# Layer 1's projections for coming units, moved to other steps of an attention unit

## The chip, the core and the metric

The kernel runs on one core of a Trainium2 chip. The core has five engines that run side by side, each with its own queue of instructions in a fixed order: TensorE (PE, matrix products, which it writes to PSUM), VectorE (DVE), ScalarE (ACT), GpSimd (POOL) and SyncE (SP, which here only issues transfers). Semaphores tie the queues together. [...] The metric is device time of one execution in microseconds.

## What is computed

Two layers act on an image of 2 x 256 x 64 x 64 in float32, that is two batches of 256 channels and 4096 places. Layer 0 is a normalised attention with four heads of 16 channels, a gate from a small convolution, and a sigmoid at its end. Layer 1, which the change touches, is

```python
qkv = jnp.einsum('oc,bchw->bohw', w_qkv, x) + b_qkv[None, :, None, None]
qkv = qkv.reshape(b, HEADS, 3 * head_dim, h * w)
q, k, v = jnp.split(qkv, 3, axis=2)
attn = jax.nn.softmax(jnp.einsum('bhdn,bhdm->bhnm', q, k) * scale, axis=-1)
out = jnp.einsum('bhnm,bhdm->bhnd', attn, v).reshape(b, c, h, w)
return jnp.einsum('oc,bchw->bohw', w_out, out) + b_out[None, :, None, None] + x
```

with four heads of 64 channels, so for each batch and head a softmax over 4096 keys for each of 4096 queries. The x here is layer 0's result.

## The kernel before

**Units.** Layer 1 works in 32 units (b, g, j): a batch b, a pair of heads g, and a block j of 512 queries. They run in that order, so unit n has n = 16 b + 8 g + j. A unit goes through the 4096 keys in 32 blocks of 128 keys, two blocks a step, thus 16 steps (`US`). Step t of the whole loop, which the code numbers on through all units, handles blocks 2t and 2t + 1; below, "step 5" is the sixth step of a unit.

**One block.** `score` (L807) makes two products, one a head, of 64 x 128 keys and 64 x 512 queries, into a pair of PSUM banks; there are two such pairs (`psp`), so the scores of a block need the pair of the block two before. `keep` takes them out: DVE folds them into a running maximum `rmax` (L824, not for the first block of a unit), and ACT copies them to SBUF as `raw` (L825). The copy stands behind the maximum. `raw` is a ring of 24 blocks.

**Groups of maxima.** The softmax uses a maximum for each query over 16 blocks (`GS`), so a unit has two groups. At a group's end, steps 8 and 16 (step 0 of the next unit), PE turns the running maximum by transposes (`turn_max`, L832), DVE reduces it (`fold`, L844), head by head through the one PSUM bank called `misc`, POOL splits the result into three bfloat16 parts (`split`, L855 to L862), PE turns those (`turn`, L871, a step later), ACT casts them (L876), and PE spreads them over the keys (`spread_shift`, L885, two steps later).

**The second half.** `LAG` is 10: ten steps after its scores, a block is shifted on DVE (L890), put through the exponential on ACT (L902), added to the row sums on POOL (`acc`, L912 for the first addition of a group, L914 after), and a step later multiplied by the values on PE (`gather`, L924). So DVE does two maxima and two shifts in a step, ACT two copies and two exps, POOL two additions, and PE four products of scores and four of values.

**The unit's end.** Steps 12 to 14 of the next unit bring the sums together on PE (`total`, L954), keep them on ACT (L962, L964), turn them and the results (`turned`, L969) and scale the results on DVE (`rows`, L995); POOL adds the halves (L1002, L1006), SP stores them (L1022).

**What comes next.** The queries of the following unit and, for the first 24 units, one block of keys and values of the next pair of heads or batch are projected in between: `next_queries` (L618, two products over the two halves of the channels, then `keep_queries` on ACT, L645), `next_keys` (L618, then `store_keys`, L760, and a store to DRAM, L763), `next_values` (L651, then `store_values`, L774, and a store, L775). Their blocks of x are fetched to one of three buffers `xb` (L614). All of them use the one `misc` bank. Units 18 to 21 carry besides, two blocks each, the output projection of the first batch: `fetch_output`, then for each half o of the output channels `project_out` (L1029, two products) and `output` (L1037 on DVE). The blocks begin at steps 0 and 8.

**The order.** It is written by hand and kept: `at(t, place, step)` hangs a piece of work on a place of a step, and the loop at the end of the kernel runs through the places. In a step PE gets the scores of both blocks, then what hangs on *early*, then the gather of two blocks, then what hangs on *late*. ACT gets the exp of the step before, the first copy, an exp, what hangs on *early end*, and the second copy. DVE gets the first maximum, a shift, *early end*, the second maximum, *late end*, and a shift. Only transfers are free to be issued ahead of this order, in SP's own queue.

Ahead of the change, a unit's extra work hangs so: step 0 maxima; 1 turning; 2 spreading; 4 and 5 keys; 6 and 7 values; 8 maxima; 9 turning; 10 spreading; 12 to 14 the unit's end; 14 *late* and 15 *early* queries. The output blocks have output 0 *early* in steps 3 and 11, output 1 *late* in 7 and 15.

Of the kernel before, what the change touches and what calls it, by code (L numbers as in the profile page):

```python
# [18 lines left out]
CC = C // P  # L19
# [8 lines left out]
def conv_attention_kernel(  # L28
# [50 lines left out]
    x1 = [  # L79
        [dram.tile([C, NB], F32, tag=f"x1_{b}_{j}", name=f"x1_{b}_{j}") for j in range(NJ)]  # L80
        for b in range(B)
    ]
# [133 lines left out]
    def at(t, place, step):  # L216
        extras.setdefault((t, place), []).append(step)
# [19 lines left out]
    with own0:  # L237
# [170 lines left out]
        def fold(u):  # L408
            seq(nc.vector.tensor_reduce(
                negmax0[u[1] % 2].rearrange("p i (h e) -> p (i h) e", e=32)[:, :, 0],  # L410
                mxs.pop(u), AX.X, ALU.max, negate=True,
            ))
# [108 lines left out]
        for n, u in enumerate(units0):  # L521
            t0 = n * NM
# [86 lines left out]
        def misc(name):  # L609
            return small_bank[0](name)  # L610

        def fetch(key, src, tag="xb", bufs=3, pool=l1x):
            t = pool.tile([P, CC, NB], F32, tag=tag, bufs=bufs, name=f"{tag}_{key}")
            nc.sync.dma_start(out=t, in_=src.rearrange("(c p) n -> p c n", p=P))  # L614
            loaded[key] = t

        def project_in(ps, xt, g, t, c):
            seq(nc.tensor.matmul(  # L618
                ps, w1[:, c, t, bass.ts(g, P)], xt[:, c, :], start=(c == 0), stop=(c == CC - 1)
            ))  # L620
# [21 lines left out]
        def keep_queries(u):  # L642
            b, g, j = u
            q, ps = qs1[u]
            seq(nc.scalar.activation(q, ps, AF.Identity, bias=b1[:, g, 0:1]))  # L645
            qs1[u] = q

        def values_in(ps, xt, g, k):

            for c in range(CC):  # L650
                seq(nc.tensor.matmul(  # L651
                    ps[:, bass.ts(k, P)], xt[:, c, bass.ts(k, P)], w1[:, c, 2, bass.ts(g, P)],
                    start=(c == 0), stop=(c == CC - 1),
                ))
# [13 lines left out]
        for i in range(NJ):  # L668
            k = (0, 0, i)
            t1 = T0 + 2 + 2 * i  # L670
# [3 lines left out]
            t1 = T0 + 20 + 3 * i if i < PB else END0 + (2, 3, 4, 9)[i - PB]  # L674
# [49 lines left out]
    with (  # L724
# [28 lines left out]
        def next_keys(b, g, i, c):  # L753
            if c == 0:
                halves_of["k"] = misc(f"k1p_{b}_{g}_{i}")
            project_in(halves_of["k"], loaded["kv", b, g, i], g, 1, c)

        def store_keys(b, g, i):
            k = l1.tile([P, NB], F32, tag="kv", name=f"k1s_{b}_{g}_{i}")
            seq(nc.scalar.activation(  # L760
                k, halves_of.pop("k"), AF.Identity, bias=b1[:, g, 1:2]
            ))
            nc.sync.dma_start(out=kd[b, g, i], in_=k)  # L763

        def next_values(b, g, i, k):
            if k == 0:
                halves_of["v"] = misc(f"v1p_{b}_{g}_{i}")
            for n in (k, k + 1):
                values_in(halves_of["v"], loaded["kv", b, g, i], g, n)

        def store_values(b, g, i):
            loaded.pop(("kv", b, g, i))
            v = l1.tile([P, NB], F32, tag="kv", name=f"v1s_{b}_{g}_{i}")
            seq(nc.scalar.copy(v, halves_of.pop("v")))  # L774
            nc.sync.dma_start(out=vd[b, g, i], in_=v)  # L775

        def load_keys(b, g, i):
            k = l1o.tile([P, NB], F32, tag=f"k{i}", name=f"k1_{b}_{g}_{i}")
            nc.sync.dma_start(out=k, in_=kd[b, g, i])
            ks[b, g, i] = k  # L780

        def load_values(b, g, i):
            v = l1o.tile([P, PB, 2, D1], F32, tag=f"v{i}", name=f"v1_{b}_{g}_{i}")
            nc.sync.dma_start(out=v.rearrange("p i h d -> p (i h d)"), in_=vd[b, g, i])
            vs[b, g, i] = v

        def next_queries(u, c):
            b, g, j = u
            if c == 0:
                q = l1x.tile([P, NB], F32, tag="q", name=f"q1_{b}_{g}_{j}")  # L790
                qs1[u] = q, misc(f"q1p_{b}_{g}_{j}")
            project_in(qs1[u][1], loaded["q", u], g, 0, c)
            if c == CC - 1:
                loaded.pop(("q", u))
# [32 lines left out]
        def turn_max(u, n, k):  # L827

            b, g, j = u
            ps = misc(f"rt_{b}_{g}_{j}_{n}_{k}")  # L830
            for i in range(PB):
                seq(nc.tensor.transpose(  # L832
                    ps[:, bass.ts(i, P)], rmax[u, n][:, k, bass.ts(i, P)], ident
                ))
            rts[k] = ps
# [123 lines left out]
        def keep_total(u):  # L959
            b, g, j = u  # L960
            row = l1.tile([P, NB], F32, tag="srow", bufs=1, name=f"srow_{b}_{g}_{j}")
            seq(nc.scalar.copy(row, srows[u]))  # L962
            srows[u] = row
            seq(nc.scalar.activation(losts[u], losts[u], AF.Exp, scale=D1**-0.5))  # L964
# [70 lines left out]
        def output(b, j, o):  # L1035
            xt = loaded["xo", b, j]
            seq(nc.vector.scalar_tensor_tensor(  # L1037
                xt[:, o, :], outs.pop((b, j, o)), bo1[:, o : o + 1], xt[:, o, :], ALU.add, ALU.add
            ))
            if o == CC - 1:  # L1040
                nc.sync.dma_start(
                    out=out[b, :, bass.ts(j, NB)].rearrange("(c p) n -> p c n", p=P), in_=xt
                )
# [11 lines left out]
        for n, u in enumerate(units):  # L1055
            b, g, j = u
            t0 = n * US
            if n > 0:
                at(t0 - 5, "start", lambda u=u, b=b, j=j: fetch(("q", u), x1[b][j]))
                at(t0 - 2, "late", lambda u=u: next_queries(u, 0))  # L1060
                at(t0 - 1, "early", lambda u=u: next_queries(u, 1))
                at(t0 - 1, "early end", lambda u=u: keep_queries(u))
            if n < len(units) - NJ:
                to = (*units[n + NJ][:2], j)
                at(t0 + 1, "start", lambda to=to: fetch(("kv", *to), x1[to[0]][to[2]]))
                for c in range(CC):
                    at(t0 + 4 + c, "early", lambda to=to, c=c: next_keys(*to, c))
                at(t0 + 5, "early end", lambda to=to: store_keys(*to))
                at(t0 + 6, "early", lambda to=to: next_values(*to, 0))
                at(t0 + 7, "early", lambda to=to: next_values(*to, 2))  # L1070
                at(t0 + 7, "early end", lambda to=to: store_values(*to))

                t1 = (n // NJ * NJ + NJ - 1) * US
                at(t1 + 2 * j + 2, "start", lambda to=to: load_keys(*to))
                at(t1 + 2 * j + 3 + LAG, "start", lambda to=to: load_values(*to))
            for k in range(NG):
                t1 = t0 + (k + 1) * GS // 2
                at(t1, "early", lambda u=u, k=k: turn_max(u, k, 0))
                at(t1, "early end", lambda u=u, k=k: fold(u, k, 0))
                at(t1, "late", lambda u=u, k=k: turn_max(u, k, 1))  # L1080
                at(t1, "late end", lambda u=u, k=k: (fold(u, k, 1), split(u, k)))
                at(t1 + 1, "late", lambda u=u, k=k: turn(u, k))
                at(t1 + 2, "early", lambda u=u, k=k: spread_shift(u, k))
            t1 = t0 + US + GS // 2
            at(t1 + 4, "early", lambda u=u: total(u))
            at(t1 + 4, "early end", lambda u=u: keep_total(u))
            at(t1 + 5, "early", lambda u=u: turn_total(u))
            at(t1 + 5, "early end", lambda u=u: factors(u))
            at(t1 + 5, "late", lambda u=u: turn_sums(u, 1))
            at(t1 + 5, "late end", lambda u=u: rows(u, 1))  # L1090
            at(t1 + 6, "early", lambda u=u: turn_sums(u, 0))
            at(t1 + 6, "early end", lambda u=u: rows(u, 0))
            if b < B - 1 and (g, j) == (PR - 1, NJ - 1):
                for i in range(NJ):
                    t1 = t0 + US + (i + 4) * GS // 2
                    at(t1, "start", lambda b=b, i=i: fetch_output(b, i))
                    for o in range(CC):
                        at(
                            t1 + 3 + 4 * o, ("early", "late")[o],
                            lambda b=b, i=i, o=o: project_out(b, i, o, misc(f"o1_{b}_{i}_{o}")),  # L1100
                        )
                        at(t1 + 3 + 4 * o, "late end", lambda b=b, i=i, o=o: output(b, i, o))

# [145 lines left out]
```

## Time and profile before

| | |
|---|---|
| median of three runs | 4754.79 us (4754.49 to 4755.42) |
| the profiled execution, its own time | 4754.21 us |
| span from its first to its last instruction | 4752.1 us |
| granted TensorE clock in it | 0.996 |
| layer 1's first copy of scores (L825) begins, the last one ends | 2071.3 and 4667.8 us of the span |
| a unit of the first 24 without output blocks (unit 10) | 2866.6 to 2947.9 us: 81.3 us |
| a unit with output blocks (unit 19) | 3604.0 to 3692.8 us: 88.8 us |
| a unit that projects only a query (unit 26) | 4193.2 to 4272.4 us: 79.2 us |

A unit's length is taken from the end of its last copy of scores to the end of the next unit's. The profile lists an instruction with its start, its duration, its engine, its source line and the tiles that it writes and reads; in square brackets stands how long the engine was idle before it and which instruction ended that wait. A busy PE is not a full PE, because its products overlap: the distance between the starts of two instructions says more than the duration of one.

### The profile page before, as it was taken

Reading aid. Unit: us, or ns where it says so; the run is one execution under the profiler, and the core shown is the slowest. Engines: PE = TensorE matmul, PEld = TensorE weight load, DVE = VectorE, ACT = ScalarE, POOL = GpSimd, SP = SyncE. Lnnn points to the kernel's source line nnn. Section 1 sums busy time; section 2 is a strip of 40 time slices with the busy share of each in tenths; the row PEclk is TensorE's granted clock in tenths of the full one; section 3 lists DMA queues with packets and bytes.
Section 4 is the critical chain, followed back from the end, with each engine's and each line's share of the span. In section 5 each row is a group of like instructions: output and inputs, shape, how many; then the busy total and the mean of one; then the engine's idle time right before and its main releaser. Section 6 shows DMA issues by size and latency. Waiting matters only on the chain.

```text
span 4752.1 us, 70463 instructions
## 1 busy us (share of the span) xinstructions
PE 4539.4 (96%) x27536; PEld 1497.5 (32%) x27536; DVE 3957.7 (83%) x4629; ACT 3399.4 (72%) x4523; POOL 2554.3 (54%) x1491
## 2 busy tenths in 40 slices
PE   8999999999999999989999999999999999999998
PEld 3433333333333333333223232323233332222222
DVE  6777777777777777459999999999999899999996
ACT  3366666666666666668888888888887778888884
POOL 5300000000000000029999999999998889999994
PEclk9999999999999999999999999999999999999999
DMA  3100000000000000110000110001111111000002
GB/s 101 35 4 19 19 19 17 15 15 14 15 15 15 14 12 17 53 61 25 16 25 23 52 32 23 25 23 36 52 33 47 62 51 45 21 14 7 14 16 73
DMA packets 105337, 139.57 MB, mean 29 GB/s; under 512 B 43884, under 2 KB 44716, under 8 KB 104892
## 3 DMA queue, kind: packets, MB, share of 16 engines
q1 hardware_dynamic: 103220, 134.61, 9.1%
q8 instruction: 216, 3.54, 0.3%
q14 instruction: 117, 0.96, 0.1%
q10 hardware_dynamic: 1784, 0.46, 0.0%
HBM read 93.33 MB, written 41.45 MB: 28 GB/s over the span
## 4 chain that ended last, share of the span: by engine, by line
PE 57%; POOL 15%; DVE 14%; issue 7%; ACT 6%; DMA 1%; SPq 0%; ACTq 0%; DVEq 0%; POOLq 0%
PE s L440 23%; POOL acc L914 13%; PE av L455 12%; DVE rmax L824 9%; PE s L807 6%; PE av L924 5%; DVE raw L890 4%; ACT raw L825 4%; PE a L402 2%; POOL acc L912 1%; PE p L262 1%; ACT raw L902 1%; PE k1p L618 1%; PE rt L832 1%; PE o L502 1%
## 5 line engine op out<-in xcount | busy, mean ns | idle before, releaser
L914 POOL TENSOR_TENSOR acc<-acc,raw 128x1024 f32<-128x1024 f32 x884 | 2097.0, 2372 | 90.8 <-ACT raw L902 31.2
L406 DVE TENSOR_REDUCE mx<-a 128x1 f32<-128x512 f32 x2048 | 1311.6, 684 | 422.5 <-PE a L402 421.3
L443 ACT ACTIVATE p<-s 128x512 f32<-128x512 f32 x2048 | 1108.2, 595 | 697.6 <-PE a L402 350.6
L807 PE MATMUL s<-q,k 64*128 64x512 f32 x4096 | 1116.9, 636 | 143.7 <-ACT raw L825 135.1
L890 DVE TENSOR_TENSOR raw<-raw,shift 128x1024 f32<-128x1024 f32 x1024 | 1236.8, 1212 | 19.5 <-PE shift L885 13.6
L824 DVE TENSOR_TENSOR rmax<-s,rmax 128x1024 f32<-128x1024 f32 x960 | 1169.1, 1218 | 72.6 <-PE s L807 70.7
L825 ACT COPY raw<-s 128x1024 f32<-128x1024 f32 x1024 | 1036.9, 1013 | 260.6 <-DVE rmax L824 170.0
L440 PE MATMUL s<-q,kT 32*128 32x512 f32 x4096 | 1215.3, 640 | 0.0
L902 ACT ACTIVATE raw<-raw 128x1024 f32<-128x1024 f32 x1024 | 1085.3, 1060 | 179.4 <-DVE raw L890 147.9
L402 PE MATMUL a<-kT,q 32*128 32x512 f32 x4096 | 1128.3, 642 | 1.8 <-DVE mx L406 1.6
L924 PE MATMUL av<-raw,v 128*64 128x512 f32 x4096 | 999.3, 606 | 2.0
L496 POOL TENSOR_TENSOR f<-f,dyn 128x512 f32<-128x512 f32 x16 | 20.2, 1266 | 1434.1 <-ACT p L443 1377.8
L455 PE MATMUL av<-p,v 128*32 128x256 f32 (+1 forms) x7904 | 650.1, 399 | 0.6 <-ACT avs L469 0.6
L807 PEld LDWEIGHTS s<-q,k 64*128 64x128 f32 x4096 | 316.9, 185 | 828.5 <-ACT raw L825 629.5
L440 PEld LDWEIGHTS s<-q,kT 32*128 32x128 f32 x4096 | 394.2, 183 | 430.2 <-issue 385.7
L924 PEld LDWEIGHTS av<-raw,v 128*64 128x64 f32 x4096 | 243.2, 136 | 587.7 <-issue 429.4
L455 PEld LDWEIGHTS av<-p,v 128*32 128x32 f32 x7904 | 157.6, 108 | 751.5 <-issue 737.2
L402 PEld LDWEIGHTS a<-kT,q 32*128 32x128 f32 x4096 | 304.4, 183 | 31.9 <-DVE mx L406 18.9
L517 POOL TENSOR_SCALAR res<-res 128x1024 f32<-128x1024 f32 x16 | 16.7, 1044 | 379.7 <-ACT res L516 379.7
L912 POOL TENSOR_TENSOR acc<-raw,raw 128x1024 f32<-128x1024 f32 x64 | 152.3, 2380 | 113.0 <-ACT raw L902 104.1
L844 DVE TENSOR_REDUCE negs<-rt 128x4 f32<-128x512 f32 x128 | 88.2, 689 | 50.2 <-PE rt L832 47.8
L310 DVE RECIPROCAL std<-std 128x128 f32<-128x128 f32 x64 | 56.1, 920 | 39.2 <-ACT std L305 39.2
(329 smaller groups left out, 1924.0 us busy)
## 6 DMA issues: line engine op xcount, KB each, us to landing
x<-in_x_dram SPq DMA_DIRECT2D x16, 512.0 KB
res<-in_x_dram SPq DMA_DIRECT2D x16, 512.0 KB
x<-res SPq DMA_DIRECT2D x16, 512.0 KB
att<-rows SPq DMA_DIRECT2D x62, 128.0 KB
kd<-k1s SPq DMA_DIRECT2D x24, 256.0 KB
vd<-v1s SPq DMA_DIRECT2D x24, 256.0 KB
k<-kd SPq DMA_DIRECT2D x24, 256.0 KB
v<-vd SPq DMA_DIRECT2D x24, 256.0 KB
```

Source lines behind the costliest of these rows:

```text
L402: seq(nc.tensor.matmul(ps, qs0[u][r, bass.ts(i, P)], kTs[b][r, bass.ts(m, NB)], start=True, stop=True,))
L406: seq(nc.vector.tensor_reduce(mxs[u][:, i * H + h, m : m + 1], ps, AX.X, ALU.max))
L440: seq(nc.tensor.matmul(ps, kTs[b][r, bass.ts(m, P)], qs0[u][r, :], start=True, stop=True))
L443: seq(nc.scalar.activation(pt[:, k, :], ps, AF.Exp, scale=D0**-0.5))
L455: seq(nc.tensor.matmul(avs[u][32 * h : 32 * h + 32, cols], vs0[b][:, m, 32 * h : 32 * h + 32], pts[t, h // 2][:, h % 2, cols], start=(m == ...
L807: seq(nc.tensor.matmul(ps[:, k, :], ks[b, g, m // PB][r, bass.ts(m % PB, P)], qs1[u][r, :], start=True, stop=True,))
L824: seq(nc.vector.tensor_tensor(rmax[u, n], ps, before, ALU.max))
L825: seq(nc.scalar.copy(raw, ps))
L890: seq(nc.vector.tensor_tensor(raws[t], raws[t], shifts[u, t % NM // GS], ALU.add))
L902: seq(nc.scalar.activation(p, p, AF.Exp, scale=D1**-0.5))
L914: seq(nc.gpsimd.tensor_tensor(accs[u, n], accs[u, n], p, ALU.add))
L924: seq(nc.tensor.matmul(avs1[u, n][k * D1 : (k + 1) * D1, :], v[:, m % PB, k, :], raws[t][:, k, :], start=(m % GS == 0), stop=(m % GS == GS ...
```

## The change

The unit's extra work hangs on other steps. Keys and values go one step forward, to steps 3 to 6, and their fetch to step 0. The next unit's queries go from steps 14 *late* and 15 *early* to 10 *late* and 11 *early*, their fetch from step 11 to step 7. In the output blocks, output 0 goes from *early* in steps 3 and 11 to *late* in steps 2 and 12, and output 1 from *late* to *early* in steps 7 and 15. No instruction is added or taken away; POOL's order is the same, and on DVE only the eight pieces of output 0 move.

```diff
             if n > 0:
-                at(t0 - 5, "start", lambda u=u, b=b, j=j: fetch(("q", u), x1[b][j]))
-                at(t0 - 2, "late", lambda u=u: next_queries(u, 0))
-                at(t0 - 1, "early", lambda u=u: next_queries(u, 1))
-                at(t0 - 1, "early end", lambda u=u: keep_queries(u))
+                at(t0 - 9, "start", lambda u=u, b=b, j=j: fetch(("q", u), x1[b][j]))
+                at(t0 - 6, "late", lambda u=u: next_queries(u, 0))
+                at(t0 - 5, "early", lambda u=u: next_queries(u, 1))
+                at(t0 - 5, "early end", lambda u=u: keep_queries(u))
             if n < len(units) - NJ:
                 to = (*units[n + NJ][:2], j)
-                at(t0 + 1, "start", lambda to=to: fetch(("kv", *to), x1[to[0]][to[2]]))
+                at(t0, "start", lambda to=to: fetch(("kv", *to), x1[to[0]][to[2]]))
                 for c in range(CC):
-                    at(t0 + 4 + c, "early", lambda to=to, c=c: next_keys(*to, c))
-                at(t0 + 5, "early end", lambda to=to: store_keys(*to))
-                at(t0 + 6, "early", lambda to=to: next_values(*to, 0))
-                at(t0 + 7, "early", lambda to=to: next_values(*to, 2))
-                at(t0 + 7, "early end", lambda to=to: store_values(*to))
+                    at(t0 + 3 + c, "early", lambda to=to, c=c: next_keys(*to, c))
+                at(t0 + 4, "early end", lambda to=to: store_keys(*to))
+                at(t0 + 5, "early", lambda to=to: next_values(*to, 0))
+                at(t0 + 6, "early", lambda to=to: next_values(*to, 2))
+                at(t0 + 6, "early end", lambda to=to: store_values(*to))
...
                     at(t1, "start", lambda b=b, i=i: fetch_output(b, i))
-                    for o in range(CC):
+                    for o, step in enumerate((t1 + (2, 4)[i % 2], t1 + 7)):
                         at(
-                            t1 + 3 + 4 * o, ("early", "late")[o],
+                            step, ("late", "early")[o],
                             lambda b=b, i=i, o=o: project_out(b, i, o, misc(f"o1_{b}_{i}_{o}")),
                         )
-                        at(t1 + 3 + 4 * o, "late end", lambda b=b, i=i, o=o: output(b, i, o))
+                        at(step, "late end", lambda b=b, i=i, o=o: output(b, i, o))
```

## The prediction

> **What bounds the kernel now.** I read the engines' shares of the whole span first, then the busy time of single units of layer 1, then who waits for whom inside one unit, then the timeline of that unit, engine by engine. The engines' line of the page:
>
> ```profile
> PE 4539.4 (96%) x27536; PEld 1497.5 (32%) x27536; DVE 3957.7 (83%) x4629; ACT 3399.4 (72%) x4523; POOL 2554.3 (54%) x1491
> ```
>
> The stretches view, one unit a row: unit 10 (a plain one), unit 19 (with output blocks), unit 26 (projects only a query):
>
> ```profile
> 2866.60:2947.90 81.30, 76.70 (x330) 24.34 (x328) 76.35 (x73) 68.45 (x75) 75.43 (x43) 1.00 0.08 24
> 3604.00:3692.80 88.80, 83.69 (x345) 27.41 (x344) 79.07 (x76) 68.67 (x74) 75.42 (x43) 1.00 0.18 57
> 4193.20:4272.40 79.20, 72.87 (x310) 21.64 (x308) 76.09 (x73) 67.92 (x72) 75.42 (x43) 1.00 0.04 11
> ```
>
> The columns are length, then busy PE, PEld, DVE, ACT and POOL. DVE is busy 76.4 of 81.3 us and POOL 75.4; nobody is full, so the unit's length is made of work plus waits. The waits of unit 10:
>
> ```profile
> PE s L807 <- ACT raw L825: 3.7, 7, 0.9
> ...
> DVE rmax L824 <- PE s L807: 2.5, 5, 0.7
> DVE negs L844 <- PE rt L832: 1.6, 2, 1.0
> ```
>
> DVE's 4.9 idle us are mostly waits for PE, and PE's own idle time is a wait for ACT to empty a score bank. So DVE sets the pace until PE is late by more than the two score banks cover. Where PE has room and where it has none, in the timeline of PE for unit 10:
>
> ```profile
> 2918.72 1.94 PE L924 MATMUL av<-raw,v 128*64 128x512 f32 x8
> 2920.59 1.13 PE L807 MATMUL s<-q,k 64*128 64x512 f32 x4
> 2922.43 1.13 PE L807 MATMUL s<-q,k 64*128 64x512 f32 x4 [0.71 <-ACT raw L825]
> 2923.49 1.94 PE L924 MATMUL av<-raw,v 128*64 128x512 f32 x8
> 2925.35 1.13 PE L807 MATMUL s<-q,k 64*128 64x512 f32 x4
> 2926.93 1.13 PE L807 MATMUL s<-q,k 64*128 64x512 f32 x4 [0.45 <-ACT raw L825]
> ...
> 2940.74 1.13 PE L618 MATMUL q1p<-b_('q', (0, 1, 3))_24142,w 128*128 128x512 f32 x2
> 2941.80 2.33 PE L807 MATMUL s<-q,k 64*128 64x512 f32 x8
> 2944.06 1.12 PE L618 MATMUL q1p<-b_('q', (0, 1, 3))_24142,w 128*128 128x512 f32 x2
> ```
>
> And the timeline of DVE, same unit:
>
> ```profile
> 2891.82 1.23 DVE L824 TENSOR_TENSOR rmax<-s,rmax 128x1024 f32<-128x1024 f32 x1 [0.66 <-PE s L807]
> ...
> 2901.98 1.23 DVE L824 TENSOR_TENSOR rmax<-s,rmax 128x1024 f32<-128x1024 f32 x1 [0.71 <-PE s L807]
> ...
> 2932.03 1.22 DVE L824 TENSOR_TENSOR rmax<-s,rmax 128x1024 f32<-128x1024 f32 x1 [0.60 <-PE s L807]
> ...
> 2942.98 1.22 DVE L824 TENSOR_TENSOR rmax<-s,rmax 128x1024 f32<-128x1024 f32 x1
> ...
> 2949.70 0.69 DVE L844 TENSOR_REDUCE negs<-rt 128x4 f32<-128x512 f32 x1 [0.98 <-PE rt L832]
> 2952.16 0.69 DVE L844 TENSOR_REDUCE negs<-rt 128x4 f32<-128x512 f32 x1 [0.63 <-PE rt L832]
> ```
>
> The reader should see two things. The second keys' and values' matmuls make DVE wait 0.66 and 0.71, but the queries at 2940 to 2945 make no maximum wait: steps 13 and 14 carry rows (2 x 0.69 us of DVE) that give PE room. And after the queries the first fold still waits 0.98 for its transposes.
>
> **The rules of the walk**, all differences of starts in unit 10: two score pairs take 0.96 each, 1.06 when the second stalled (2922.43 to 2923.49); a query or key matmul 1.05; four value products 1.09; the gather 1.87 (2918.72 to 2920.59); a maximum can start 1.18 after its scores (2890.64 to 2891.82); DVE's pair of maximum and shift is 2.26; ACT starts a copy 0.07 after the maximum ends and takes 1.01, an exp 1.06, a kept query 0.67; the scores two blocks on need that copy.
>
> **Keys and values one step earlier** (steps 3 to 6; nothing added or removed). Walked from 2882.15, where PE waits 0.64 for a copy: first key product 2883.21, gather 2884.26, scores 2886.13, so the first maximum of step 4 starts 2887.31 instead of 2886.55. Second key product, gather, scores 2890.97: step 5's at 2892.15 against 2891.82. The stored keys (0.68 on ACT) delay a copy, the scores after it start 2892.31, the values follow: step 6 starts 2897.51 (2896.66), step 7 2902.39 (2901.98). Step 7 is now free and PE catches up: step 8 starts 2906.92 against 2906.85, and the second fold at 2911.22 against 2911.07. So the free step returns nearly all, and **+0.15 us** remains. Units without keys and values support that the fold gains nothing by a free step 7: their steps 8 and 9 take together 10.58 us between the copies that end them, as in unit 10.
>
> **Queries in steps 10 and 11.** *Late* in step 10, the first product stands between gather and the next scores: 2920.74 (0.15 late), scores 2921.80, maximum of block 22 at 2922.98 against 2922.30, +0.68. The second follows the scores of 23: gather 2924.78, scores 2926.65, block 24 at 2927.83 (2926.82), +1.01. The kept query (0.67) pushes the copy of 23 to 2926.92, so the scores of 25 start 2927.99; the sums' 1.0 us of PE come right behind, scores of 26 at 2931.92, block 26 at 2933.10 (2932.03), +1.07. ACT, which has to keep the sums too, hands over the scores of 27 at 2932.95, and the turned results reach rows 1.14 late. PE had 0.71 and 0.45 of room here; 2.1 us are put into it.
>
> **What leaving steps 14 and 15 gives back.** DVE runs without a gap from 2933 to 2949, so it stays 1.14 behind. Without the kept query the copy of 31 starts straight behind its maximum (2947.69), scores 2948.76, transposes 2949.82, fold 2950.52 against 2949.70. Of 1.14, 0.32 is returned: **+0.82**, 0.80 by the second fold. Step 2's shift follows a chain of copy, scores and spread that moves by the same 0.80. POOL's splitting, which sits behind its accumulations at 2955.57, moves to about 2956.0 and stays ahead of that chain. A plain unit gains 0.80 us of length; one with the queries alone, walked the same way from the looser step 10 of unit 26, 0.62.
>
> **Output blocks** (units 18 to 21, two blocks each). Before, output 1 *late* in steps 7 and 15 makes DVE wait 2.5 and 2.6 us for it; output 0 *early* in 3 and 11 costs some 1.2 to 1.6. The four cost 88.75 - 81.30 = 7.45 a unit. Now output 1 is *early* in a step with no projection: 1.92 of PE ahead of the gather, its 0.75 of DVE after the second maximum finds it ready; the walk gives 1.5 and 1.1. Output 0 becomes *late* in steps 2 and 12, and inherits the wait: 1.5 us of DVE idle in step 2, 2.6 in step 12 behind sums and gather. Walked together: step 2 with 7 costs 2.75 (before 3.9), step 12 with 15 costs 4.46 with the queries (before 3.6 with them). Net -0.1 a unit; bounds -2.5 (neither late wait) and +2.5 (both at full 2.6).
>
> **Queues.** SP's fetches run a whole unit ahead: the query issued at 2903.91 belongs to the unit after next, held back only until a buffer is read. A key fetch now stands ahead of the stores of finished rows, but waits for a buffer that the query's second product frees in step 11, before the rows of step 14 exist. The block of attention for output 0 is issued at 3605.20; SP's traffic of that step is over by 3614, and the earlier use comes at least 14 us after the issue. POOL's order is untouched; its two gaps a unit (2.55 and 0.90) cover exps up to a microsecond late. If that cover went, the ring of 24 blocks would hold ACT's copies, as it does once already by 0.62 at 2936.09.
>
> [...]
>
> **Sum.** Units 1 to 17, 22 and 23: 19 x 0.80 = 15.2. Units 24 to 30: 7 x 0.62 = 4.3. Units 18 to 21: -0.4. Units 0 and 31: nothing (0 has little in steps 10 to 15, 31 has no next query). Together +19.1 on the profiled execution's 4754.21, that is 4773.3; the median is 0.6 higher, so **4774**.
>
> **Rivals.**
> - *Queries hide, so it ends faster.* If PE's idle 0.94, 0.71 and 0.45 in steps 10 to 12 swallow the two products, nothing is lost there and the first fold comes 0.46 earlier (the kept query, 0.67 on ACT, no longer delays copy 31). 31 x -0.46 + 23 x 0.15 = -11: 4743. It decides if block 26 is less than 0.4 late. Against it: the wait of 0.60 at 2932.03 exists already.
> - *POOL paces, no change.* POOL is busy 75.4 us and its ring holds ACT at 2921.36 and 2936.09. If that ring sets the unit's length, DVE's delay is only moved into it and 0.2 a unit remains: 4760. Against it: POOL idles 3.4 us a unit.
> - *More is lost.* If the late exps also starve POOL and the splitting of the second maxima follows late, no recovery of 0.32 comes and the key move costs what step 4 shows (0.76): 24 x 0.76 + 31 x 1.1 = 52 at the most, likelier half: 4790.
>
> **How the numbers follow.** Forecast 0.70, hidden queries 0.08, POOL 0.10, more lost 0.12. 0.2% is 9.5 us, about what a measurement can tell. The forecast's own range: 0.35 us a unit of error on 27 units and 2.5 on four gives about 4760 to 4786; it reaches to 4789 for half of the last rival. Faster 0.08, same 0.10, slower 0.82.
>
> **What would show it.** In the changed profile, DVE's maxima wait for PE in steps 11, 12 and 13 by 0.5, 0.3 and 0.7; the first fold's wait shrinks from 0.98 to about 0.65; plain units last 82.1, units 24 to 30 79.8, output units 88.7. A plain unit below 81.3, or an accumulation ending most of ACT's waits, would prove me wrong.

## The result, and the profile after

The changed kernel takes **4764.93 us** (median; 4763.12 to 4768.81) against 4754.73 (4752.77 to 4757.61) for the kernel before in the same sessions: a ratio of 1.0023, with a 95% interval of 1.0016 to 1.0030. It is 10.2 us slower. The forecast was 4774, so the sign and the mechanism are as forecast and the time is 9 us too long: the loss is a little over half of the 19 us that were forecast. The profiled execution of the changed kernel took 4768.81 us (span 4766.7), the longest of its times; what it has beyond the median is looked at in the last section.

The engines' line of the page:

```profile
PE 4537.6 (95%) x27536; PEld 1501.6 (32%) x27536; DVE 3959.3 (83%) x4629; ACT 3408.6 (72%) x4523; POOL 2555.5 (54%) x1491
```

The counts of instructions are those of before. The busy times of PE and DVE, the two engines on the path, differ by 2 us, one down and one up; ACT's is 9 us longer, but that counts overlapping instructions once: added up one by one, the same 4523 instructions last 4.8 us longer than before (3608.3 us against 3603.5), and in `e_keep`, an experiment below that is as slow as the changed kernel, 0.5 us shorter. So the 10 us are waits and not work. The stretches view, for the same three units (10, 19 and 26; length, then busy PE, PEld, DVE, ACT and POOL):

```profile
2874.10:2956.00 81.90, 76.51 (x328) 24.41 (x328) 76.52 (x74) 68.70 (x74) 75.49 (x43) 1.00 0.08 23
3615.90:3704.00 88.10, 83.30 (x348) 27.37 (x344) 78.95 (x77) 69.00 (x74) 75.45 (x43) 1.00 0.18 57
4204.40:4284.00 79.60, 72.60 (x308) 21.71 (x308) 76.11 (x74) 68.14 (x72) 75.51 (x43) 1.00 0.04 11
```

Taken exactly, from the end of a unit's last copy of scores to the end of the next unit's, and over all units of a kind:

| unit | before | after | difference | forecast |
|---|---|---|---|---|
| plain (19 units) | 81.29 | 81.82 | +0.53 | +0.80 |
| query alone (7 units, 24 to 30) | 79.19 | 79.59 | +0.40 | +0.62 |
| with output blocks (4 units; 19 and 20 stand for them) | 88.75 | 88.13 | -0.62 | -0.1 |

19 x 0.53 + 7 x 0.40 - 4 x 0.62 = +10.4, which agrees with the measured 10.2. The single units at the edges differ: an output block in step 15 acts on the next unit, so unit 18 is 0.14 longer and unit 22, a plain one, 0.23 shorter. In the sum these cancel: units 1 to 31 of the two profiles differ by +10.3.

The waits inside unit 10, 2874.1 to 2956.0 (who waited for whom; sum, times, longest):

```profile
PE s L807 <- ACT raw L825: 4.6, 8, 1.2
...
DVE rmax L824 <- PE s L807: 3.2, 7, 0.7
...
DVE negs L844 <- PE rt L832: 1.5, 3, 0.7
```

DVE's waits for scores grew from 2.5 us to 3.2, and its waits for transposes shrank by 0.1 (there is one more of them, 0.24 at the first group's second fold). PE's own wait for ACT, 3.7 before, is 4.6: PE is late first and later finds the score banks full. The timeline of PE where the queries now are, and later where they were:

```profile
2926.38 1.94 PE L924 MATMUL av<-raw,v 128*64 128x512 f32 x8
2928.24 1.12 PE L618 MATMUL q1p<-b_('q', (0, 1, 3))_24023,w 128*128 128x512 f32 x2
2929.30 1.99 PE L807 MATMUL s<-q,k 64*128 64x512 f32 x8
2931.22 1.12 PE L618 MATMUL q1p<-b_('q', (0, 1, 3))_24023,w 128*128 128x512 f32 x2
2932.27 1.94 PE L924 MATMUL av<-raw,v 128*64 128x512 f32 x8
2934.14 1.13 PE L807 MATMUL s<-q,k 64*128 64x512 f32 x4
2935.45 1.13 PE L807 MATMUL s<-q,k 64*128 64x512 f32 x4 [0.18 <-ACT raw L825]
...
2939.37 2.06 PE L807 MATMUL s<-q,k 64*128 64x512 f32 x8
...
2943.82 0.65 PE L969 MATMUL turned<-ident,avs 128*128 128x128 f32 x4
...
2951.50 1.13 PE L807 MATMUL s<-q,k 64*128 64x512 f32 x4 [1.18 <-ACT raw L825]
```

Before, PE stood idle for 0.71 and 0.45 us in this stretch; now 0.18 is left. At the end of the unit, in the place that the queries left, it stands idle for 1.18. The timeline of DVE in the same unit (two maxima of the keys' and values' steps, then blocks 22, 24 and 26, the first rows, and the first fold):

```profile
2894.84 1.23 DVE L824 TENSOR_TENSOR rmax<-s,rmax 128x1024 f32<-128x1024 f32 x1 [0.68 <-PE s L807]
...
2905.01 1.23 DVE L824 TENSOR_TENSOR rmax<-s,rmax 128x1024 f32<-128x1024 f32 x1 [0.71 <-PE s L807]
...
2930.47 1.23 DVE L824 TENSOR_TENSOR rmax<-s,rmax 128x1024 f32<-128x1024 f32 x1 [0.44 <-PE s L807]
...
2935.32 1.23 DVE L824 TENSOR_TENSOR rmax<-s,rmax 128x1024 f32<-128x1024 f32 x1 [0.23 <-PE s L807]
...
2940.55 1.23 DVE L824 TENSOR_TENSOR rmax<-s,rmax 128x1024 f32<-128x1024 f32 x1 [0.62 <-PE s L807]
...
2944.51 0.69 DVE L995 TENSOR_TENSOR rows<-turned,f 128x512 f32<-128x512 f32 x1
...
2957.76 0.69 DVE L844 TENSOR_REDUCE negs<-rt 128x4 f32<-128x512 f32 x1 [0.65 <-PE rt L832]
```

The waits at blocks 22, 24 and 26 are 0.44, 0.23 and 0.62 where 0.5, 0.3 and 0.7 were forecast; the first two are new, the third was 0.60 before. The fold's wait is 0.65, as forecast. The rows at 2944.51 wait for nothing, and there the forecast was wrong: it had them held up.

How late each start is against before, both timelines laid on each other at step 2 of unit 10 (the tables of blocks below are made in the same way):

| start on DVE | forecast | measured |
|---|---|---|
| block 8 (step 4, second keys) | +0.76 | +0.76 |
| blocks 20, 21 (keys and values long past) | +0.15 | +0.13 |
| block 22 | +0.68 | +0.65 |
| block 24 | +1.01 | +0.97 |
| block 26 | +1.07 | +0.99 |
| block 28, behind the rows | +1.14 | +0.97 |
| block 30 | +1.14 | +0.86 |
| first fold | +0.82 | +0.53 |

### The profile page after: what moved, and what is told of

Same layout as the page of the kernel before. It is cut to its first block, busy times and chain, and to the rows that moved or that the text cites. A ratio compares the mean times of both kernels' runs of the same rounds, so it can differ in the third digit from the quotient of the medians.

```text
span 4766.7 us, 70452 instructions
## 1 busy us (share of the span) xinstructions
PE 4537.6 (95%) x27536; PEld 1501.6 (32%) x27536; DVE 3959.3 (83%) x4629; ACT 3408.6 (72%) x4523; POOL 2555.5 (54%) x1491
## 4 chain that ended last, share of the span: by engine, by line
PE 63%; DVE 18%; issue 8%; ACT 6%; POOL 3%; DMA 0%; ACTq 0%; DVEq 0%; POOLq 0%
PE s L440 23%; PE av L455 12%; DVE rmax L824 12%; PE s L807 9%; PE av L924 7%; DVE raw L890 5%; ACT raw L825 5%; POOL acc L914 3%; PE a L402 2%; ACT raw L902 1%; PE rt L832 1%; PE p L262 1%; PE k1p L618 1%; PE o L502 1%; PE v1p L651 1%
```

## The experiments

The theory is the forecast's: each plain unit loses what two query products ahead of blocks 22 to 26 push DVE back by, less what the emptied step 15 returns. The rivals: POOL's ring sets the pace; the queries cost nothing and something else moved was dear (the output blocks); or the loss can be had back by mending a single link. Lengths of units are from the profiles, times are medians with the kernel before measured beside them.

### The two halves of the change

`e_keys` has the first half of a unit as after and the second as before; `e_queries` the other way round. The edits in words:

```diff
 e_keys, against the kernel before
+ fetch of x for keys at t0; keys at t0 + 3, t0 + 4; values at t0 + 5, t0 + 6
+ output blocks that start at step 0: output 0 late in step 2, output 1 early in 7
  queries late in 14, early in 15; output blocks that start at step 8 in 11 and 15
 e_queries, against the kernel before
+ fetch for queries at t0 - 9, queries late in step 10, early in 11
+ output blocks that start at step 8: output 0 late in step 12, output 1 early in 15
  keys 4 and 5, values 6 and 7; output blocks that start at step 0 in 3 and 7
```

> The first half of a unit as in the changed kernel (keys and values in steps 3 to 6, output blocks that begin at step 0 moved), the second half as before (queries in 14 and 15, the other output blocks unmoved). If the queries carry the cost: 23 units x 0.13 = +3, four output halves x -1.2 = -5, and up to +2 in unit 0, so 4753 to 4757, with plain units of 81.42 us. If the keys and values carry it: about 4765.

> The second half of a unit as in the changed kernel (queries in 10 and 11, output blocks that begin at step 8 moved), the first half as before. If the queries carry the cost: 30 units x 0.40 = +12, output halves +0.6, so 4766 to 4768, with plain units of 81.70 and units 24 to 30 of 79.59. If the keys and values carry it: about 4755.

| | time | ratio | plain | query alone | with output |
|---|---|---|---|---|---|
| `e_keys` | 4753.34 (before 4754.59) | 0.9998 (0.9989 to 1.0007) | +0.12 | -0.02 | -1.18 |
| `e_queries` | 4766.21 | 1.0025 (1.0015 to 1.0034) | +0.39 | +0.38 | +0.53 |

The halves add up: -1.25 + 11.62 = 10.4 against 10.2. The keys and values cost 0.12 a unit, as walked (0.15), and the output blocks of this half give 1.18 back, as walked (2.75 - 3.9 = -1.15). All of the loss lies in the second half.

### No query products at all

`e_none` is the kernel before without the projection of queries for units 1 to 31: all of them use the first unit's queries, so that part of the computation is left out.

```diff
-                at(t0 - 5, "start", lambda u=u, b=b, j=j: fetch(("q", u), x1[b][j]))
-                at(t0 - 2, "late", lambda u=u: next_queries(u, 0))
-                at(t0 - 1, "early", lambda u=u: next_queries(u, 1))
-                at(t0 - 1, "early end", lambda u=u: keep_queries(u))
+                at(t0 - 1, "early end", lambda u=u: qs1.update({u: qs1[units[0]]}))
```

> The kernel before without the projection of queries for units 1 to 31, which all use the first unit's queries; everything else is unchanged. If emptying step 15 lets the first fold of the second maxima start earlier, as the walk has it (0.46 of its wait of 0.98): 31 x -0.46, about 4740, plain units 80.85. If the fold's wait has another cause (the chain from the last maximum, or POOL behind it): no change, 4755, plain units 81.3.

It took 4736.08 us, a ratio of 0.9962 (0.9949 to 0.9974). A plain unit is 0.46 shorter, one with the query alone 0.47, one with output blocks 1.15. Two folds of it, in the timeline of DVE for unit 10:

```profile
2945.32 0.69 DVE L844 TENSOR_REDUCE negs<-rt 128x4 f32<-128x512 f32 x1 [0.65 <-PE rt L832]
...
2947.77 0.69 DVE L844 TENSOR_REDUCE negs<-rt 128x4 f32<-128x512 f32 x1 [0.63 <-PE rt L832]
```

The first fold comes 0.46 earlier than in the kernel before: 0.33 because its wait falls from 0.98 to 0.65, and 0.11 because block 30 already comes that much earlier. So the queries' projection, two products and the keeping, costs 0.46 a unit in steps 14 and 15. That is the gain on which the rival *queries hide* was built, and it is really there; what the rival lacked is what the new place costs, 0.85 at block 26 in `e_queries`.

### The keeping of the queries alone, the second product alone, both

The forecast names two things behind block 24's lateness: the second product itself, which PE does ahead of the scores of block 24, and ACT's keeping of the queries, which pushes the copy of block 23 and so the scores of 25 and 26. `e_keep` takes the keeping out of the way, `e_half` leaves the second product out (half of the channels of x are then missing from the queries of units 1 to 31), `e_both` does both. All are edits of the changed kernel.

```diff
 e_keep and e_both
-                at(t0 - 5, "early end", lambda u=u: keep_queries(u))
+                at(t0 - 5, "late end", lambda u=u: keep_queries(u))
 e_half and e_both
-                at(t0 - 5, "early", lambda u=u: next_queries(u, 1))
 (the first product then starts and stops its bank by itself)
```

> The changed kernel with the kept queries behind the second copy of step 11 instead of ahead of it; PE's products stay in 10 late and 11 early. If the delay at block 26 is made of PE's two products and of ACT's piece that pushes a copy by 0.45: block 26 comes 0.35 earlier and most of that reaches the fold, 31 x -0.3, about 4756, plain units 81.5. If it is PE's products alone: 4765, plain units 81.82.

> The changed kernel with the kept queries behind the second copy of step 11, and without the second of the two query products (step 11 early): queries come from half the channels, which is left out on purpose. Against the run with the kept queries moved, the one edit is 1.05 us of PE less in step 11. If PE's second product is what makes block 24 late by 0.97: block 22 stays at +0.65, block 24 falls to +0.65 and the fold loses 0.3 less, 31 x -0.3 = -10, about 4755, plain units 81.5. If the first product alone sets the delay: 4764 as with both.

The first sentence of the expectation for `e_half` does not fit the kernel that ran: that kernel kept its queries at the *early end*, as the changed kernel does. The combination that the sentence speaks of is `e_both`, run after it.

> The changed kernel with both edits at once: the kept queries behind the second copy of step 11, and no second query product in step 11 (queries from half the channels; the second half is left out). Each edit alone left the fold's delay where it was: with the product gone block 26 stayed 0.99 late by way of ACT's copy, with the kept queries moved block 28 stayed 0.96 late by way of block 24 and ACT. If these are two paths beside each other, both have to go: block 24 to 28 at +0.65, plain units 81.4 to 81.5, about 4754. If the first product in step 10 late alone sets the delay: 81.74, 4762.

| | time (before beside it) | ratio | plain | block 22 | 24 | 26 | 28 | 30 |
|---|---|---|---|---|---|---|---|---|
| changed kernel | 4764.93 (4754.73) | 1.0023 (1.0016 to 1.0030) | +0.53 | +0.65 | +0.97 | +0.99 | +0.97 | +0.86 |
| `e_keep` | 4764.38 | 1.0022 (1.0013 to 1.0032) | +0.51 | +0.65 | +0.97 | +0.65 | +0.96 | not taken |
| `e_half` | 4762.66 | 1.0017 (1.0008 to 1.0026) | +0.45 | +0.65 | +0.66 | +0.99 | +0.91 | not taken |
| `e_both` | 4755.40 (4755.03) | 1.0002 (0.9993 to 1.0011) | +0.21 | +0.65 | +0.65 | +0.65 | +0.65 | +0.55 |

`e_keep` was expected at 4756 and `e_half` at 4755; neither gained what it should have. DVE in `e_keep`, unit 10 (blocks 22, 24 and 26, and the rows):

```profile
2925.90 1.23 DVE L824 TENSOR_TENSOR rmax<-s,rmax 128x1024 f32<-128x1024 f32 x1 [0.44 <-PE s L807]
...
2930.74 1.23 DVE L824 TENSOR_TENSOR rmax<-s,rmax 128x1024 f32<-128x1024 f32 x1 [0.23 <-PE s L807]
...
2935.64 1.23 DVE L824 TENSOR_TENSOR rmax<-s,rmax 128x1024 f32<-128x1024 f32 x1 [0.28 <-PE s L807]
...
2939.92 0.69 DVE L995 TENSOR_TENSOR rows<-turned,f 128x512 f32<-128x512 f32 x1 [0.34 <-PE turned L969]
```

Block 26 waits 0.28 instead of 0.62, as expected; but two instructions later the rows wait 0.34 for the turned results, which the changed kernel has no wait for. The 0.34 won is lost again in full. DVE in `e_half` (blocks 22 and 26; its lines from the edit on are one higher):

```profile
2928.36 1.23 DVE L825 TENSOR_TENSOR rmax<-s,rmax 128x1024 f32<-128x1024 f32 x1 [0.44 <-PE s L808]
...
2938.43 1.22 DVE L825 TENSOR_TENSOR rmax<-s,rmax 128x1024 f32<-128x1024 f32 x1 [0.94 <-PE s L808]
```

Here block 24 gains 0.31, and block 26 waits 0.94 instead of 0.62. And with both edits, the same two blocks in `e_both`:

```profile
2923.14 1.23 DVE L825 TENSOR_TENSOR rmax<-s,rmax 128x1024 f32<-128x1024 f32 x1 [0.43 <-PE s L808]
...
2932.88 1.22 DVE L825 TENSOR_TENSOR rmax<-s,rmax 128x1024 f32<-128x1024 f32 x1 [0.60 <-PE s L808]
```

The 0.60 is what the kernel before has at block 26 (0.60 at 2932.03): nothing is lost behind block 22 any more. So two paths of nearly the same length run from step 11 to step 14 (with one cut, block 28 is still 0.96 or 0.91 late). One goes through DVE's late block 24, ACT's copy of it, the scores of 27 and the turned results to the rows; the other through ACT's keeping, the copy of 23 and the scores behind it to block 26. Each edit cuts one, and the other then sets nearly the same end. With both cut, DVE stays at the 0.65 of block 22; less the 0.11 and the 0.33 that the old place gives back, this is the +0.21 of its plain unit.

### Rivals: POOL, and the output blocks

`e_pool` leaves two of every 15 additions of the row sums out on POOL, so the sums of those blocks are missing. `e_out` puts output 1 of the changed kernel *late* again.

```diff
 e_pool
-            if on_tensor(t):
+            if on_tensor(t) or m % GS in (5, 11):
 e_out
-                            step, ("late", "early")[o],
+                            step, "late",
```

> The changed kernel with two of the fifteen additions of each group left out on POOL (their blocks are missing from the row sums): 4 x 2.45 = 9.8 us of POOL less in a unit. If PE's lateness and DVE's pace make the unit: nothing, 4763 to 4765, plain units 81.8. If POOL and its ring of 24 blocks set the pace: up to -2 us a unit, 4700 to 4745.

> The changed kernel with output 1 of the eight output blocks late in steps 7 and 15 again, as before the change. If being late makes DVE wait for it (2.5 us before) and early lets it be ready: +1.1 for each of eight, about 4774, units 19 to 21 of 90.3. If the place within the step does not matter once the step is free of projections: 4765, 88.1.

`e_pool`: 4764.77 us, a ratio of 1.0021 (1.0012 to 1.0030), and a plain unit of 81.81 against the changed kernel's 81.82. Taking work from POOL moves nothing, so POOL's ring is not the pace of the changed kernel. For the kernel before there is a sign that speaks for this rival: of the chain of work that ended last, followed back from the last instruction, its page gives 15% of the span to POOL, and that of the changed kernel 3%. No run takes work from POOL there, but `e_none` leaves POOL's additions as they are and is still 0.46 a unit shorter, so they alone did not set the length there either.

`e_out`: 4767.83, a ratio of 1.0028 (1.0017 to 1.0038), and 88.91 for an output unit against 88.12. It was expected at 4774 with units of 90.3, so the miss is large: *late* costs 0.79 a unit where 2.2 was expected. The lost 0.79 lies nearly all behind step 7 (step 8 takes 7.30 us instead of 6.58); behind step 15, steps 0 and 1 of the next unit take 6.75 + 5.10 instead of 5.95 + 5.83, which is the same within 0.1. DVE around output 1 of units 19 and 20 (step 7 of unit 19; then step 15 and the folds behind it) says why. First `e_out`:

```profile
3655.74 0.75 DVE L1037 SCALAR_TENSOR_TENSOR xo_('xo', 0, 2)_28203<-o,bo,xo_('xo', 0, 2)_28203 128x512 f32<-128x512 f32 x1 [1.40 <-PE o L1029]
...
3701.78 0.75 DVE L1037 SCALAR_TENSOR_TENSOR xo_('xo', 0, 3)_28447<-o,bo,xo_('xo', 0, 3)_28447 128x512 f32<-128x512 f32 x1 [1.60 <-PE o L1029]
...
3704.70 0.68 DVE L844 TENSOR_REDUCE negs<-rt 128x4 f32<-128x512 f32 x1
3705.68 1.23 DVE L824 TENSOR_TENSOR rmax<-s,raw 128x1024 f32<-128x1024 f32 x1 [0.29 <-ACT raw L825]
3706.82 0.68 DVE L844 TENSOR_REDUCE negs<-rt 128x4 f32<-128x512 f32 x1
```

And the changed kernel:

```profile
3660.29 1.23 DVE L824 TENSOR_TENSOR rmax<-s,rmax 128x1024 f32<-128x1024 f32 x1 [0.69 <-PE s L807]
...
3702.85 0.75 DVE L1037 SCALAR_TENSOR_TENSOR xo_('xo', 0, 3)_28447<-o,bo,xo_('xo', 0, 3)_28447 128x512 f32<-128x512 f32 x1
...
3707.04 0.69 DVE L844 TENSOR_REDUCE negs<-rt 128x4 f32<-128x512 f32 x1 [1.19 <-PE rt L832]
...
3709.49 0.69 DVE L844 TENSOR_REDUCE negs<-rt 128x4 f32<-128x512 f32 x1 [0.63 <-PE rt L832]
```

In a step without projections the *late* waits are 1.40 and 1.60 and not 2.5 and 2.6. And the *early* place has waits of its own: 0.69 for the next scores behind step 7, and 1.19 + 0.63 at the two folds behind step 15. So *late* loses 1.40 - 0.69 = 0.71 in the one place and 1.60 + 0.29 - 1.82 = 0.07 in the other, together the 0.79 of a unit.

### The waits that are left: transposes half a step earlier

In a plain unit DVE waits for the transposes of the maxima at the two folds that end the unit: 0.98 and 0.63 us in unit 10 of the kernel before, 0.65 and 0.64 in the changed kernel, 0.65 and 0.63 in `e_none`, `e_keep`, `e_half` and `e_both`. `e_turn` takes `e_keys` and puts the first head's transposes behind the second gather of the step before (its fold then comes ahead of the next step's first maximum), and the second head's in place of the first's; `e_aturn` does the same to the changed kernel.

```diff
-                at(t1, "early", lambda u=u, k=k: turn_max(u, k, 0))
-                at(t1, "early end", lambda u=u, k=k: fold(u, k, 0))
-                at(t1, "late", lambda u=u, k=k: turn_max(u, k, 1))
+                at(t1 - 1, "late", lambda u=u, k=k: turn_max(u, k, 0))
+                at(t1, "early", lambda u=u, k=k: (fold(u, k, 0), turn_max(u, k, 1)))
                 at(t1, "late end", lambda u=u, k=k: (fold(u, k, 1), split(u, k)))
```

> Keys, values and the output blocks of step 0 as in the changed kernel, queries as before, and both turns of a group's maxima half a step earlier: the first transposes late in the step before, the first fold ahead of the next step's first maximum, the second transposes early, the second fold late end as it was. If a fold's wait for the transposes behind the next scores costs time: 0.4 to 0.9 at the second maxima of each unit, 4725 to 4742. If POOL's splitting, in its fixed place, holds what follows anyway: 4753, as without this edit.

> The changed kernel, queries in 10 and 11, with the turns of the maxima half a step earlier as in the fastest version. If the free step 15 is worth something once the first transposes go there: the fold's wait goes and about as much is gained as with the queries in 14 and 15, 4749 and plain units 81.1. If the queries' delay in steps 11 to 13, which came back in part through the fold's wait, then stays whole: 4753 or more, plain units 81.3.

| | time (before beside it) | ratio | plain | query alone | with output |
|---|---|---|---|---|---|
| `e_turn` | 4738.49 (4754.31) | 0.9964 (0.9951 to 0.9978) | 80.74 | 78.6 | 87.73 |
| `e_aturn` | 4743.35 (4755.03) | 0.9975 (0.9965 to 0.9985) | 81.04 | 78.9 | 87.45 |

**`e_turn` beats both kernels**, by 16 us the one before and by 26 the changed one. `e_aturn` came out 6 us below the lower of its two expectations, 4749. DVE at the folds of unit 10 in `e_turn`:

```profile
2943.49 0.69 DVE L844 TENSOR_REDUCE negs<-rt 128x4 f32<-128x512 f32 x1 [0.15 <-PE rt L832]
2944.10 1.21 DVE L890 TENSOR_TENSOR raw<-raw,shift 128x1024 f32<-128x1024 f32 x1
2945.66 1.23 DVE L824 TENSOR_TENSOR rmax<-s,raw 128x1024 f32<-128x1024 f32 x1 [0.35 <-ACT raw L825]
2946.80 0.68 DVE L844 TENSOR_REDUCE negs<-rt 128x4 f32<-128x512 f32 x1
```

And PE there (the transposes, then the turning of POOL's split maxima):

```profile
2942.80 0.66 PE L832 MATMUL rt<-ident,rmax 128*128 128x128 f32 x4
2943.38 1.99 PE L807 MATMUL s<-q,k 64*128 64x512 f32 x8
2945.30 0.66 PE L832 MATMUL rt<-ident,rmax 128*128 128x128 f32 x4
...
2952.51 0.40 PE L871 MATMUL nm1p<-ident,negmax 128*128 128x128 bf16 x4 [0.90 <-POOL negmax L858]
```

The first fold's wait falls from 0.98 to 0.15, and the second has none. A plain unit is 0.67 shorter than in `e_keys` (81.41 to 80.74), and 0.78 shorter than in the changed kernel (81.82 to 81.04). Part of what the folds give is lost in new places: DVE waits 0.35 for ACT's copy ahead of the next maximum, and PE waits 0.90 for POOL's splitting (0.5 before); what this second wait costs was not tried. Between `e_turn` and `e_aturn` the queries' place makes 4.9 us, 0.30 a plain unit (81.04 - 80.74). So the place in steps 14 and 15 stays the better one when the folds no longer wait.

## Why the prediction was right, and where its size was off

**What bounds the kernel.** Right. DVE's chain paces the unit and PE costs time where it comes late to it; no instruction was added, and 10 us went into DVE's waits. That POOL does not pace is shown by `e_pool` for the changed kernel (81.81 against 81.82 us a plain unit); for the one before, `e_none`, 0.46 a unit shorter with the same additions on POOL, speaks against it.

**Keys and values, +0.15 a unit.** Right: 0.12 alone, and 0.76 at block 8 to the hundredth. The free step returns nearly all of it.

**Queries in steps 10 and 11.** Right up to block 26: +0.65, +0.97, +0.99 against the walked 0.68, 1.01, 1.07.

**The step that failed in size** is "the turned results reach rows 1.14 late", and with it "DVE runs without a gap from 2933 to 2949, so it stays 1.14 behind". Rows start 0.97 late and wait for nothing. The term that was too large in the walk is the scores of 27, for which PE was to wait for ACT until 2932.95: in the changed kernel they follow the scores of 26 without a wait (the row of eight at 2939.37), at 2932.80 on the scale of before, and the transposes for the rows start 0.98 late. The path through block 24 and ACT's copy of it ends at about that same time, as `e_keep` shows by coming out at 0.96 on that path alone. Then, DVE does not stay that far behind: at block 30 it is 0.86 late. The first fold shows why: in the kernel before the queries in step 14 held up block 30 by 0.11, which I had counted as no wait at all; `e_none`, without them, has block 30 earlier by 0.11. So the delay carried to the end is 0.86 and not 1.14. The return at the fold, 0.32, was right (0.33), and 0.86 - 0.33 = 0.53 is the plain unit. Of the 0.28 by which the walk was too large, 0.17 are the rows' and 0.11 block 30's. 0.27 too much on 19 units, 0.22 on seven: 6.7 of the 9 us.

**Output blocks.** The four halves were walked well: `e_keys` shows -1.18 for the first half (2.75 - 3.9 = -1.15), and in the changed kernel the four blocks' places cost 88.13 - 81.82 = 6.3 over a plain unit. But "net -0.1 a unit" is a slip of arithmetic: its own figures, 2.75 - 3.9 and 4.46 - 3.6, make -0.29. With the queries' share 0.26 too large as in a plain unit, -0.55 would have stood there; -0.62 is measured. That is the rest of the 9 us, 4 x 0.5 = 2. `e_out` shows one more thing: the wait of 2.6 us for a *late* output 1 in step 15 was read as a price, and in the changed order moving it away from that place is worth 0.07, because DVE then waits 1.82 at the folds.

**Queues.** Nothing, as forecast: in unit 10 no engine's wait ends on a transfer. SP itself stands waiting, 23.0 us of it for the query's products to free a buffer, as described.

**Rivals.** *Queries hide* falls by its own point: block 26 is 0.99 late, not below 0.4; its 0.46 exists and is outweighed. *POOL paces* falls with `e_pool`, though its 4760 lay nearer to the result than the forecast's 4774 did. *More is lost* falls: the recovery of 0.33 comes. Its price of 4790 was also off by its own sum, since half of 52 us makes 4781; and the range counts 27 units where 19 and seven are 26.

With no instruction added or taken away, the order alone is worth +10.2 us (the change) and -15.8 us (`e_turn`) against the kernel before.

What stays open: how much of `e_turn`'s gain POOL's splitting holds back was not tried, and neither was the effect of less work on POOL in the kernel before.

## What to carry to other kernels

When a piece of work of a fixed order is moved, walk the chain of starts on the pacing engine through both places, and subtract what the old place had cost: that place may hold up more than the one instruction at which a wait is printed (here block 30 by 0.11 us besides the fold's 0.33). An edit that shortens one of two parallel paths of nearly equal length shows little (4764.4 and 4762.7 us against 4764.9), and both together show what it is worth (4755.4); a null result of one edit is no proof that its path does not matter. And before work is moved away from a wait, look at whether the awaited instruction itself can go earlier: eight transposes a group did more (-15.8 us) than any place of the queries.

## What the hardware showed besides

In unit 0 of the changed kernel's profiled execution the granted TensorE clock fell to half in the midst of work. The stretches view there (the last columns are granted clock, DMA share and GB/s):

```profile
2100.00:2103.00 3.00, 2.22 (x11) 1.18 (x10) 1.43 (x2) 1.01 (x1) 0.00 (x0) 0.72 0.00 0
2103.00:2108.00 5.00, 4.87 (x17) 1.70 (x17) 3.11 (x4) 2.03 (x2) 0.88 (x4) 0.50 0.00 2
2108.00:2112.00 4.00, 3.56 (x14) 1.10 (x16) 2.74 (x3) 2.52 (x3) 0.00 (x0) 0.98 0.00 0
```

And PE's timeline around it:

```profile
2099.77 1.13 PE L807 MATMUL s<-q,k 64*128 64x512 f32 x4 [1.80 <-ACT raw L825]
...
2103.36 3.79 PE L807 MATMUL s<-q,k 64*128 64x512 f32 x8
```

Eight products take 3.79 us instead of 1.99. The spell lasted 6.83 us, from 2101.31 to 2108.14, after PE had waited 1.80 us; a wait of 0.78 lies in the spell. Unit 0 takes 65.6 us, and 63.0 in `e_keep` and `e_pool`. Other profiles have such a spell in the same unit at another place or none: 3.41 us at 2111.3 in `e_keys`, 6.83 at 2100.3 in `e_half`, none there in `e_keep` and `e_pool`, which have the keys and values of unit 0 where the changed kernel has them and the same wait of 1.80 us (ending at 2096.9 and 2097.6). So the order does not settle it, and it is 2.6 of the 3.9 us by which the profiled execution lies above the median.

Between the clock's rise at 2084.24 and this fall the granted clock was 1.00, and the longest idle time of PE in that stretch was the 1.80 us that end at 2099.77. What sets the start and the length of such a spell is not shown by any run here.
